# Graph attention on one core: GpSimd multiplies the mask into the last chunk of every other unit, and the projection beside the second attention takes its steps in another order

## The chip, the cores and the metric

The kernel runs on one core of a Trainium2 chip. A core has five engines that run at the same time, each with its own queue in program order: TensorE (PE; its weight loads are listed as PEld), VectorE (DVE), ScalarE (ACT), GpSimd (POOL) and SyncE (SP), which issues transfers. The metric is the device time of one execution in microseconds.

## The reference, cut to what matters

Four layers work on a graph of 3327 nodes with 512 features and a sparse 0/1 matrix `adj`. Layers 0, 2 and 3 are graph attentions with 8 heads of 64 features, layer 1 is a mean over neighbours with dense products. Each starts with a layer norm and ends with a residual sum.

```python
def _L3_gnn_ref(h, adj, W, a):
    hp = jnp.einsum('nd,hdf->hnf', h, W)
    f_src = jnp.einsum('hnf,hf->hn', hp, a_src)
    f_dst = jnp.einsum('hnf,hf->hn', hp, a_dst)
    e = jax.nn.leaky_relu(f_src[:, :, None] + f_dst[:, None, :], ALPHA)
    e = jnp.where(adj[None] > 0, e, NEG_FILL)
    att = jax.nn.softmax(e, axis=-1)
    out = jnp.einsum('hij,hjf->hif', att, hp)
    ...
    return jax.nn.elu(out)

x = x + _L0_gnn_ref(relu(layernorm(x)), adj, ...)   # attention, batch norm
x = x + _L1_gnn_ref(relu(layernorm(x)), adj, ...)   # mean over neighbours
x = x + _L2_gnn_ref(relu(layernorm(x)), adj, ...)   # attention, elu
x = x + _L3_gnn_ref(relu(layernorm(x)), adj, ...)   # attention, elu
```

(The layer norm and relu are written short here.)

## The kernel before, in words

The nodes are padded to 3328, 26 blocks of 128. The kernel first builds, from `adj`, a list of neighbours for each group of 64 target nodes: 52 groups, and for each so many chunks of 128 neighbour indices as the table `CAPS` gives it, 359 chunks in all. Everything after that works on these lists and not on the dense matrix.

A table in device memory holds one row per node: for each head its 64 projected features and a factor (the exponential of its score, so that the sum of weights falls out as a 65th column), and 8 numbers, one per head, for the maximum below. Layer 0's rows also carry the packed edge bits. A second, small array `r_dram` holds the factors of the target nodes.

`attend` runs one attention. It is called three times, for layers 0, 2 and 3; the text calls these the first, second and third attention. It goes through units of two or three chunks (`UNIT` is 3), 135 units in an attention. For each unit:

- `load` (L1165 is the gather in it) issues on GpSimd one indirect transfer per chunk, 128 table rows into the tile `rows`, which has six buffers.
- DVE computes `mx` (L1266): the larger of the target's factor `r_bc`, which TensorE has spread over the partitions in PSUM, and the row's number. 512 elements per partition and chunk: 8 heads by 64 targets. `mx` is a tile in PSUM with one buffer.
- DVE computes `wgt` (L1273): `mx` times the mask, 64 bytes per partition and chunk, the same for all heads. The result is in SBUF and has three buffers.
- TensorE multiplies (L1287): per chunk and head `wgt` transposed by the features, summed in PSUM in `facc` over the group's chunks.
- `later` takes one step of every group that is ending (L1215 copies the sums, L1219 takes reciprocals, L1225 scales the features) and calls `tick`, which takes one or two steps of the work beside the attention.

In the first attention `load` also makes the mask: DVE takes the edge bits out of the gathered rows ("on", L1252) and ACT turns them into 0 and 1 (L1258). The later attentions use the mask that was kept.

The order of PE, DVE and ACT inside `attend` is the program's own (`manual_schedule`); GpSimd isn't in that list, and the only instructions that `attend` gives it are gathers, in the order of the units. A gather waits until TensorE and DVE have finished with the buffer that it overwrites.

Beside the second attention runs the projection of the next layer, `Following.rest`, a generator that `tick` advances, block by block: transposes of the normed rows and `hT` on ACT (L845, L848), the scores `p_sd` (L853) with three ACT operations on them (L857, L858, L860), the clamp of `s_col` on DVE (L863) and the product `p_wh` on TensorE (L866), then `halves` and eight row multiplies on ACT (L870) and the table's row out through SP, then a transpose of `halves`' result (L874), and last its copy `r_row` (L877) and its transfer. `halves` makes two ACT operations (L730, L731) and returns a function that makes a subtraction on DVE (L734). All PSUM tiles of the projection share one buffer (`p_ps`).

Of the kernel before, what the change touches and what calls it, by code (L numbers as in the profile page):

```python
# [23 lines left out]
F32 = mybir.dt.float32  # L24
# [3 lines left out]
I32 = mybir.dt.int32  # L28
# [4 lines left out]
ALU = mybir.AluOpType  # L33
ET = mybir.EngineType
# [4 lines left out]
P = 128  # L39
H = 8  # L40
F = 64
# [9 lines left out]
GB = 64  # L51
# [4 lines left out]
LNB = 5  # L56
ROW = H * (F + 1) + H
UNIT = 3
SUNIT = 2
SROWS = 8  # L60
SAHEAD = 2
SMALL = 53.0
# [662 lines left out]
def halves(nc, pool, cs, sf):  # L725


    rf = pool.tile([P, H], F32, name="r_full", tag="r_full", bufs=2)
    rs = pool.tile([P, 2, H], F32, name="r_half", tag="r_half", bufs=2)
    nc.scalar.activation(rf, sf, AF.Exp, scale=0.8, bias=cs["down"])  # L730
    nc.scalar.copy(rs.bitcast(F32R)[:, 0, :], rf)  # L731

    def other():
        nc.vector.tensor_tensor(rs.bitcast(F32R)[:, 1, :], rf, rs[:, 0, :], ALU.subtract)  # L734
        return rs.rearrange("p t h -> p (t h)")

    return other


class Following:  # L740
# [100 lines left out]
    def rest(self, c, hx):  # L841
        nc, pp, WA, wl = self.tc.nc, self.pool, self.WA, self.wl
        tp = self.psum.tile([P, KC, P], F32, name="p_ps", tag="p_ps", bufs=self.pb)
        for kc in range(KC):
            nc.tensor.transpose(tp[:, kc, :], hx[:, kc * P : (kc + 1) * P], self.cs["ident"])  # L845
        hT = pp.tile([P, KC, P], F32, name="hT", tag="hT", bufs=2)
        for kc in range(KC):
            nc.scalar.activation(hT[:, kc, :], tp[:, kc, :], AF.Relu, accum_out=self.hs[:, c, kc : kc + 1])  # L848
        yield True
        self.mean(c, hT)  # L850
        sd = self.psum.tile([P, BANK], F32, name="p_sd", tag="p_ps", bufs=self.pb)
        for kc in range(KC):
            nc.tensor.matmul(sd[:, : 2 * H], hT[:, kc, :], WA[wl][:, kc, :], start=(kc == 0), stop=(kc == KC - 1))  # L853
        row = pp.tile([P, ROW], F32, name="v_row", tag="v_row", bufs=2)
        V = row[:, : H * (F + 1)].rearrange("p (h f) -> p h f", f=F + 1)
        d = sd[:, H : 2 * H]
        nc.scalar.activation(V[:, :, F : F + 1], d.rearrange("p (h o) -> p h o", o=1), AF.Exp)  # L857
        nc.scalar.activation(row[:, H * (F + 1) :], d, AF.Exp, scale=-0.8, bias=self.cs["down"])  # L858
        sf = pp.tile([P, H], F32, name="s_col", tag="s_col", bufs=2)
        nc.scalar.copy(sf, sd[:, :H])  # L860
        yield True

        nc.vector.tensor_scalar(sf, sf, -SMALL, SMALL, ALU.max, ALU.min)  # L863
        wh = self.psum.tile([P, D], F32, name="p_wh", tag="p_ps", bufs=self.pb)
        for kc in range(KC):
            nc.tensor.matmul(wh, hT[:, kc, :], self.Wt[:, kc, :], start=(kc == 0), stop=(kc == KC - 1))  # L866
        yield True
        rs = halves(nc, pp, self.cs, sf)
        for h in range(H):
            nc.scalar.mul(V[:, h, 0:F], wh[:, h * F : (h + 1) * F], V[:, h, F : F + 1])  # L870
        nc.sync.dma_start(self.table[c * P : (c + 1) * P, :ROW], row.bitcast(I32))
        yield True
        tr = self.psum.tile([2 * H, P], F32, name="p_tr", tag="p_ps", bufs=self.pb)
        nc.tensor.transpose(tr, rs(), self.cs["ident"])  # L874
        yield True
        rr = pp.tile([2 * H, P], F32, name="r_row", tag="r_row", bufs=2)
        nc.scalar.copy(rr, tr)  # L877
        n = P // GB
        nc.sync.dma_start(
            self.r_dram[c * n : (c + 1) * n, :, :, :].rearrange("g t h i -> (t h) g i"),  # L880
            rr.rearrange("h (g i) -> h g i", i=GB),
        )
        yield None
# [253 lines left out]
def sparse(ctx: ExitStack, tc: tile.TileContext, t: dict, out: bass.AP, WA, ls, cs, idx, rdeg, first):  # L1137
# [5 lines left out]
    nc = tc.nc  # L1143
# [18 lines left out]
    mask = keep.tile([P, NCH, GB], U8, name="mask")  # L1162
# [7 lines left out]
    def attend(layer, table, r_dram, finish, tick=lambda: None, home=None):  # L1170
# [5 lines left out]
        units = []  # L1176
        for g in range(ls.G):
            mine = list(ls.batches(g, UNIT))
            units += [(g, k0, n, i == 0, i == len(mine) - 1) for i, (k0, n) in enumerate(mine)]
        hq = H // PG  # L1180
        sw = hq * (F + 1)
        with tc.tile_pool(name=f"fatt{layer}", bufs=2) as ap, tc.tile_pool(
            name=f"facc_ps{layer}", bufs=2, space=PSUM
        ) as aps, tc.manual_schedule(engines={ET.PE, ET.DVE, ET.Activation}):
            rows, rrs, rbs, accs, ends = {}, {}, {}, {}, []

            def fetch(g):
# [43 lines left out]
            def later():  # L1231
                for e in list(ends):
                    if next(e, 0) == 0:
                        ends.remove(e)
                tick()
# [4 lines left out]
            def load(i):  # L1240

                if i >= len(units):
                    return
                g, k0, n, _, _ = units[i]
                gi = ap.tile([P, UNIT, width], I32, name="rows", tag="rows", bufs=6)
                rows[i] = gi.bitcast(F32)
                for k in range(n):
                    gather(gi[:, k, :], table, k0 + k)
                if layer == 0:
                    nw = GB // WB  # L1250
                    on = ap.tile([P, UNIT, nw, WB], U16, name="on", tag="on")
                    nc.vector.tensor_tensor(  # L1252
                        on[:, :n],
                        gi[:, :n, ROW:].bitcast(U16)[:, :, g * nw : (g + 1) * nw].unsqueeze(3).to_broadcast([P, n, nw, WB]),
                        cs["bit"].unsqueeze(1).unsqueeze(1).to_broadcast([P, n, nw, WB]),
                        ALU.bitwise_and,
                    )
                    nc.scalar.activation(mask[:, k0 : k0 + n, :], on[:, :n].rearrange("p k w b -> p k (w b)"), AF.Sign)  # L1258

            load(0)  # L1260
            for i, (g, k0, n, begins, stops) in enumerate(units):
                gt = rows.pop(i)
                mk = mask[:, k0 : k0 + n, :]
                full = [P, n, H, GB]
                mx = aps.tile([P, UNIT, H, GB], F32, name="mx", tag="mx", bufs=1)
                nc.vector.tensor_tensor(  # L1266
                    mx[:, :n],
                    rbs[g].unsqueeze(1).to_broadcast(full),
                    gt[:, :n, H * (F + 1) : ROW].unsqueeze(3).to_broadcast(full),
                    ALU.max,  # L1270
                )
                wt = ap.tile([P, UNIT, H, GB], F32, name="wgt", tag="wgt", bufs=3)
                nc.vector.tensor_tensor(wt[:, :n], mx[:, :n], mk.unsqueeze(2).to_broadcast(full), ALU.mult)  # L1273
                load(i + 1)
                later()
                if begins:
                    fetch(g + 2)
                    acc = aps.tile([P, BANK], F32, name="facc", tag="acc")
                    accs[g] = acc
                    spread(g + 1)  # L1280

                for k in range(n):
                    f, l = begins and k == 0, stops and k == n - 1
                    for q in range(hq):
                        for v in range(PG):
                            h = q * PG + v
                            nc.tensor.matmul(  # L1287
                                accs[g][v * GB : (v + 1) * GB, q * (F + 1) : (q + 1) * (F + 1)],
                                wt[:, k, h, :],
                                gt[:, k, h * (F + 1) : (h + 1) * (F + 1)],  # L1290
                                start=(f and q == 0),
                                stop=(l and q == hq - 1),
                            )
                if stops:
                    ends.append(ending(g))
# [34 lines left out]
    with ExitStack() as mx:  # L1330
# [150 lines left out]
        def tick():  # L1481
            for e in list(ends):
                if next(e, 0) == 0:
                    ends.remove(e)
            proj.tick()
# [3 lines left out]
        for b in range(NB):  # L1489
            ps = list(zip_longest(*(list(ls.batches(b * PG + u, SUNIT)) for u in range(PG))))  # L1490
            parts += [(b, p, i == 0, i == len(ps) - 1) for i, p in enumerate(ps)]
        loaded = {}

        def load(i):
# [3 lines left out]
            for u, kn in enumerate(parts[i][1]):  # L1498
                if kn is not None:
                    k0, n = kn  # L1500
                    zt = gp.tile([P, SUNIT, D], F32, name="z_rows", tag="z_rows", bufs=SROWS)
                    mf = gp.tile([P, SUNIT, GB], F32, name="z_mask", tag="z_mask", bufs=SROWS)
                    nc.scalar.copy(mf[:, :n, :], mask[:, k0 : k0 + n, :])  # L1503
# [7 lines left out]
        for i, (b, _, begins, stops) in enumerate(parts):  # L1511
# [4 lines left out]
            for r, u, k, m, z in loaded.pop(i):  # L1516
# [3 lines left out]
                g = b * PG + u  # L1520
# [102 lines left out]
```

## Time and profile before

| what | value |
| --- | --- |
| runs | 2900.37, 2915.10, 2917.88 us; median 2915.1 us |
| profiled execution, its own time | 2553.76 us |
| its span, first to last instruction | 2551.8 us |
| mean granted TensorE clock in it | 0.851 |
| busy PE, DVE, ACT, POOL | 1825.0, 1852.3, 1068.3, 1387.4 us |

The profiled execution was shorter than the runs beside it; sums made from its rows are compared with its own time. Its rows name a line, an engine, an operation, the tile written and the tiles read, and then a count, the busy time and the mean in ns, and the idle time of that engine just ahead of these instructions with what ended it ("issue": nothing that the profile shows). In the table by stretches the columns are the stretch and its length, then busy time and count for PE, weight loads, DVE, ACT and POOL, the granted clock, the share of the DMA engines and GB/s. In a timeline they are start, duration, engine, line and instruction, and in brackets the idle time before it.

### The profile page before, as it was taken

What the parts mean: (1) busy time and instruction counts of PE and PEld (TensorE: products, weight loads), DVE (VectorE), ACT (ScalarE), POOL (GpSimd) and SP (SyncE); (2) the same over time, 40 slices, a digit from 0 to 9 for tenths busy, and PEclk for the clock granted to TensorE, in tenths of its full rate; (3) what the DMA queues carried; (4) which work ended last, traced back from release to release, by engine and by line L of the source; (5) the groups of instructions that cost most, each with busy time, mean ns of one, the idle gap of its engine ahead of it and who ended that gap; (6) DMA issues with size and microseconds to landing.
All of it is one profiled execution on the core that took longest, in us unless ns stands there. A gap on an engine that the chain in (4) does not pass through costs nothing.

```text
span 2551.8 us, 53690 instructions
## 1 busy us (share of the span) xinstructions
PE 1825.0 (72%) x21112; PEld 1161.8 (46%) x21112; DVE 1852.3 (73%) x2272; ACT 1068.3 (42%) x3810; POOL 1387.4 (54%) x1482
## 2 busy tenths in 40 slices
PE   3667756776677698889999657778878646566653
PEld 2444444454454342223333356656555435555543
DVE  7667579999997850222333499999877279999996
ACT  4553212333445332334455214667766601233444
POOL 1000176777772026777777277776554067777672
PEclk9767889988888899999999778897877787777787
DMA  8773198888783566788888478887665178888784
GB/s 326 288 263 123 43 296 276 280 281 260 241 253 95 191 217 198 234 247 260 254 267 255 125 223 242 235 240 232 199 200 177 39 215 232 236 238 243 232 238 123
DMA packets 189057, 562.57 MB, mean 220 GB/s; under 512 B 37764, under 2 KB 42304, under 8 KB 185470
## 3 DMA queue, kind: packets, MB, share of 16 engines
q0 software_dynamic: 115456, 404.86, 53.3%
q1 hardware_dynamic: 73342, 154.20, 17.0%
q8 instruction: 169, 2.77, 0.4%
q14 instruction: 90, 0.74, 0.1%
HBM read 499.26 MB, written 59.68 MB: 219 GB/s over the span
## 4 chain that ended last, share of the span: by engine, by line
PE 30%; DVE 24%; issue 13%; ACT 9%; DMA 8%; POOL 3%; DVEq 0%; SPq 0%; POOLq 0%; ACTq 0%
DVE mx L1266 12%; PE facc L1287 8%; DVE wgt L1273 8%; PE sage_acc L1522 4%; DMA z_rows<-h_dram,idx 4%; PE p_wh L866 4%; DMA rows<-table,idx 3%; PE n_ps L1471 3%; PE p_wh L808 3%; ACT fhp L1225 2%; POOL z_rows L1165 2%; PE s_ps L1445 2%; POOL rows L1165 1%; ACT bn_y L1225 1%; ACT v_row L870 1%
## 5 line engine op out<-in xcount | busy, mean ns | idle before, releaser
L1165 POOL DMA_INDIRECT rows<-table,idx x1077 | 1027.7, 954 | 580.0 <-issue 224.5
L1287 PE MATMUL facc<-rows,wgt 128*64 128x65 f32 x17232 | 722.5, 253 | 393.7 <-DVE wgt L1273 259.7
L1287 PEld LDWEIGHTS facc<-rows,wgt 128*64 128x64 f32 x17232 | 667.1, 165 | 518.2 <-DVE wgt L1273 310.5
L1266 DVE TENSOR_TENSOR mx<-r_bc,rows 128x1536 f32<-128x1536 f32 (+1 forms) x405 | 639.4, 1579 | 48.4 <-DMA fin_x<-fx 17.7
L1273 DVE TENSOR_TENSOR wgt<-mx,mask 128x1536 f32<-128x1536 f32 (+1 forms) x405 | 638.4, 1576 | 42.3 <-DVE mx L1266 1.0
L1165 POOL DMA_INDIRECT z_rows<-h_dram,idx x359 | 340.7, 949 | 273.7 <-ACT hT L1442 141.0
L1225 ACT ACTIVATE fhp<-sums,rd 64x64 f32<-64x64 f32 x832 | 219.9, 334 | 305.4 <-DVE rd L1219 302.0
L1522 PE MATMUL sage_acc<-z_rows,z_mask 128*64 128x512 f32 x718 | 209.8, 618 | 33.0 <-DMA z_rows<-h_dram,idx 32.6
L1258 ACT ACTIVATE mask<-on 128x192 uint8<-128x192 uint16 (+1 forms) x135 | 46.5, 345 | 325.3 <-DVE on L1252 321.8
L1086 POOL DMA_DIRECT2D list_b<-shift x12 | 6.0, 503 | 271.7 <-DVE shift L1040 271.5
L811 DVE TENSOR_TENSOR sd_pr<-p_wh,ab 128x1024 f32<-128x1024 f32 x26 | 31.8, 1225 | 141.4 <-PE p_wh L808 141.4
L1522 PEld LDWEIGHTS sage_acc<-z_rows,z_mask 128*64 128x64 f32 x718 | 52.2, 137 | 156.2 <-issue 77.6
L680 PE MATMUL wh_ps<-fWt,hT 128*128 128x512 f32 x208 | 123.3, 748 | 0.0
L866 PE MATMUL p_wh<-fWt,hT 128*128 128x512 f32 x208 | 117.2, 714 | 1.4 <-ACT s_col L860 1.4
L1225 ACT ACTIVATE bn_y<-sums,rd 64x64 f32<-64x64 f32 x416 | 109.5, 333 | 2.4 <-DVE rd L1219 0.5
L1503 ACT CAST z_mask<-mask 128x128 f32<-128x128 uint8 (+1 forms) x196 | 52.7, 284 | 118.7 <-PE sage_acc L1522 117.5
L1476 DVE TENSOR_TENSOR s_o<-n_ps,bn_y 128x512 f32<-128x512 f32 x26 | 17.9, 690 | 116.2 <-PE n_ps L1471 116.2
L1215 ACT COPY sums<-facc 128x260 f32<-128x260 f32 x156 | 56.6, 363 | 104.7 <-DMA rows<-table,idx 77.7
L1471 PE MATMUL n_ps<-fWx,aT 128*128 128x512 f32 x208 | 98.7, 608 | 0.0
L808 PE MATMUL p_wh<-fWt,hT 128*128 128x512 f32 x208 | 96.9, 610 | 2.0 <-DVE hT L699 1.9
L1445 PE MATMUL s_ps<-fWx,hT 128*128 128x512 f32 x208 | 93.5, 603 | 3.4 <-ACT hT L1442 3.4
L1198 PE MATMUL r_bc<-r_two,fones 2*128 2x512 f32 x156 | 89.1, 575 | 6.6 <-DMA r_two<-r_dram 3.6
(213 smaller groups left out, 2146.3 us busy)
## 6 DMA issues: line engine op xcount, KB each, us to landing
adj_i<-in_adj SPq DMA_DIRECT2D x26, 1664.0 KB
table<-v_row SPq DMA_DIRECT2D x78, 264.0 KB
rows<-table,idx POOLq DMA_INDIRECT x1077
fin_x<-fx SPq DMA_DIRECT2D x52, 256.0 KB
ln_x<-in_x SPq DMA_DIRECT2D x26, 256.0 KB
bn_x<-in_x SPq DMA_DIRECT2D x13, 512.0 KB
fx<-bn_x SPq DMA_DIRECT2D x13, 512.0 KB
fsage_x<-fx SPq DMA_DIRECT2D x26, 256.0 KB
```

The source lines that it names most:

```text
L680: nc.tensor.matmul(wh, hT[:, kc, :], self.Wt[:, kc, :], start=(kc == 0), stop=(kc == KC - 1))
L808: nc.tensor.matmul(wh, hT[:, kc, :], self.Wt[:, kc, :], start=(kc == 0), stop=(kc == KC - 1))
L866: nc.tensor.matmul(wh, hT[:, kc, :], self.Wt[:, kc, :], start=(kc == 0), stop=(kc == KC - 1))
L1165: nc.gpsimd.indirect_dma_start(out=dst, out_offset=None, in_=src[:, :], in_offset=bass.IndirectOffsetOnAxis(ap=idx[:, k : k + 1], axis=0))
L1198: nc.tensor.matmul(rb, ones[0:2, :].bitcast(F32R), rrs.pop(g).bitcast(F32R), start=True, stop=True)
L1225: nc.scalar.mul(hp[o0 : o0 + GB, h * F : (h + 1) * F], sm[mine, q, 0:F], rd[mine, q, :])
L1266: nc.vector.tensor_tensor(mx[:, :n], rbs[g].unsqueeze(1).to_broadcast(full), gt[:, :n, H * (F + 1) : ROW].unsqueeze(3).to_broadcast(full), ...
L1273: nc.vector.tensor_tensor(wt[:, :n], mx[:, :n], mk.unsqueeze(2).to_broadcast(full), ALU.mult)
L1287: nc.tensor.matmul(accs[g][v * GB : (v + 1) * GB, q * (F + 1) : (q + 1) * (F + 1)], wt[:, k, h, :], gt[:, k, h * (F + 1) : (h + 1) * (F + 1)],
L1445: nc.tensor.matmul(ps, hT[:, kc, :], Wx[:, 0, kc, :], start=(kc == 0), stop=(kc == KC - 1))
L1471: nc.tensor.matmul(ps, aT[:, kc, :], Wx[:, 1, kc, :], start=(kc == 0), stop=(kc == KC - 1))
L1522: nc.tensor.matmul(acc[u * GB : (u + 1) * GB, :], m, z, start=f, stop=l)
```

## The change

It does two things. In `attend`, for every unit with an odd number, the last chunk's maximum is written by DVE into `wgt` directly, and GpSimd multiplies it there by the mask, of which ACT has made an fp32 copy (`mask_f`) one unit ahead. The other chunks of that unit go through `mx` and `wgt` on DVE as before. GpSimd's instructions in `attend` are now in the program's own order. The gathers of three units (`AHEAD`) are issued before the first unit, and those of unit i + 3 at the beginning of unit i. The making of the mask is cut out of `load` and stays where `load(i + 1)` was.

In `Following.rest`, which runs beside the second attention, the work of a block is cut differently: the clamp of `s_col` goes behind the product, `halves` behind the row multiplies, its subtraction gets a step alone, and the transpose goes into the step of `r_row`.

```diff
+AHEAD = 3
...
         yield True
-
-        nc.vector.tensor_scalar(sf, sf, -SMALL, SMALL, ALU.max, ALU.min)
         wh = self.psum.tile([P, D], F32, name="p_wh", tag="p_ps", bufs=self.pb)
         for kc in range(KC):
             nc.tensor.matmul(wh, hT[:, kc, :], self.Wt[:, kc, :], start=(kc == 0), stop=(kc == KC - 1))
         yield True
-        rs = halves(nc, pp, self.cs, sf)
+
+        nc.vector.tensor_scalar(sf, sf, -SMALL, SMALL, ALU.max, ALU.min)
         for h in range(H):
             nc.scalar.mul(V[:, h, 0:F], wh[:, h * F : (h + 1) * F], V[:, h, F : F + 1])
         nc.sync.dma_start(self.table[c * P : (c + 1) * P, :ROW], row.bitcast(I32))
+        rs = halves(nc, pp, self.cs, sf)
+        yield True
+        rs = rs()
         yield True
         tr = self.psum.tile([2 * H, P], F32, name="p_tr", tag="p_ps", bufs=self.pb)
-        nc.tensor.transpose(tr, rs(), self.cs["ident"])
-        yield True
+        nc.tensor.transpose(tr, rs, self.cs["ident"])
         rr = pp.tile([2 * H, P], F32, name="r_row", tag="r_row", bufs=2)
         nc.scalar.copy(rr, tr)
...
-        ) as aps, tc.manual_schedule(engines={ET.PE, ET.DVE, ET.Activation}):
+        ) as aps, tc.manual_schedule(engines={ET.PE, ET.DVE, ET.Activation, ET.Pool}):
...
-                if layer == 0:
+
+            def edges(i):
+
+                if layer == 0 and i < len(units):
+                    g, k0, n, _, _ = units[i]
+                    gi = rows[i].bitcast(I32)
...
-            load(0)
+            mps = {}
+
+            def widened(i):
+
+                if i < len(units) and i % 2:
+                    _, k0, n, _, _ = units[i]
+                    mp = mps[i] = ap.tile([P, GB], F32, name="mask_f", tag="mask_f", bufs=3)
+                    nc.scalar.copy(mp, mask[:, k0 + n - 1, :])
+
+            for i in range(AHEAD):
+                load(i)
+            edges(0)
             for i, (g, k0, n, begins, stops) in enumerate(units):
+                load(i + AHEAD)
                 gt = rows.pop(i)
                 mk = mask[:, k0 : k0 + n, :]
+                wt = ap.tile([P, UNIT, H, GB], F32, name="wgt", tag="wgt", bufs=3)
+
+                if i % 2:
+                    n -= 1
+                    one = [P, H, GB]
+                    nc.vector.tensor_tensor(
+                        wt[:, n], rbs[g], gt[:, n, H * (F + 1) : ROW].unsqueeze(2).to_broadcast(one), ALU.max
+                    )
+                    nc.gpsimd.tensor_tensor(wt[:, n], wt[:, n], mps.pop(i).unsqueeze(1).to_broadcast(one), ALU.mult)
+                    mk = mk[:, :n, :]
                 full = [P, n, H, GB]
                 mx = aps.tile([P, UNIT, H, GB], F32, name="mx", tag="mx", bufs=1)
...
-                wt = ap.tile([P, UNIT, H, GB], F32, name="wgt", tag="wgt", bufs=3)
                 nc.vector.tensor_tensor(wt[:, :n], mx[:, :n], mk.unsqueeze(2).to_broadcast(full), ALU.mult)
-                load(i + 1)
+                edges(i + 1)
                 later()
+                widened(i + 1)
...
+                n = units[i][2]
                 for k in range(n):
```

## The prediction

> **What bounds the kernel now.** I read four things in this order: the page's slices, the groups by line, the engines' timelines inside one attention stage, and the waits of the second attention. The slices first.
>
> ```profile
> DVE  7667579999997850222333499999877279999996
> POOL 1000176777772026777777277776554067777672
> ```
>
> Slices are 63.8 us. In slices 5 to 12, 22 to 30 and 32 to 39, the three attentions, VectorE (DVE) is at nine tenths and GpSimd (POOL) seems to have a quarter of its time free. The table by stretches says the same, in the page's order PE, weight loads, DVE, ACT, POOL:
>
> ```profile
> 319.00:800.00 481.00, 325.29 (x5892) 237.20 (x5892) 451.48 (x457) 168.65 (x593) 341.28 (x359) 0.87 0.83 263
> 1447.00:1985.00 538.00, 404.89 (x6117) 309.90 (x6117) 470.30 (x476) 304.57 (x1180) 342.63 (x359) 0.80 0.73 216
> 2046.00:2552.00 506.00, 285.05 (x5796) 251.31 (x5796) 461.24 (x374) 158.15 (x520) 343.75 (x359) 0.77 0.76 221
> ```
>
> So 359 gathers in each attention and a DVE with 30 to 68 us idle. The groups give the price of the pieces: the two DVE operations of a unit at 1536 (three chunks) and 1024 elements (two), and the gather.
>
> ```profile
> L1165 POOL DMA_INDIRECT rows<-table,idx x1077 | 1027.7, 954 | 580.0 <-issue 224.5 <-PE facc L1287 149.9 <-DMA r_two<-r_dram 111.6
> L1266 DVE TENSOR_TENSOR mx<-r_bc,rows 128x1536 f32<-128x1536 f32 x267 | 470.1, 1761 | 47.3 <-DMA fin_x<-fx 17.7 <-DMA rows<-table,idx 13.3 <-PE r_bc L1198 11.5
> L1266 DVE TENSOR_TENSOR mx<-r_bc,rows 128x1024 f32<-128x1024 f32 x138 | 169.3, 1227 | 1.2
> ```
>
> The reader is to stop at "issue 224.5" in the first row: idle time in which GpSimd waited for nothing. The timeline of GpSimd in the third attention shows what it is:
>
> ```profile
> 2213.67 1.23 DVE L1273 TENSOR_TENSOR wgt<-mx,mask 128x1024 f32<-128x1024 f32 x1
> 2214.81 0.17 DVE L1219 RECIPROCAL rd<-sums 128x4 f32<-128x4 f32 x1
> 2214.99 1.77 DVE L1266 TENSOR_TENSOR mx<-r_bc,rows 128x1536 f32<-128x1536 f32 x1
> ```
>
> ```profile
> 2212.93 0.94 POOL L1165 DMA_INDIRECT rows<-table,idx  x1 [0.30 <-PE facc L1287]
> 2214.18 0.95 POOL L1165 DMA_INDIRECT rows<-table,idx  x1 [0.30 <-DMA rows<-table,idx]
> 2215.43 0.95 POOL L1165 DMA_INDIRECT rows<-table,idx  x1 [0.31 <-PE facc L1287]
> 2216.68 0.95 POOL L1165 DMA_INDIRECT rows<-table,idx  x1 [0.30 <-issue]
> ```
>
> Gathers start every 1.25 us, with a hole of 0.30 or 0.31 us whatever releaser is named. GpSimd runs back to back. The first and last gather of each attention start at 319.43 and 788.18, 1447.72 and 1978.16, 2046.52 and 2513.65: 468.8, 530.4 and 467.1 us, where 358 spacings of 1.25 us make 447.5. The true slack of GpSimd is therefore 21.3, 82.9 and 19.6 us, 123.8 in all. **GpSimd and DVE are both bounds** of the first and third attention, within 5% of each other. In the second, small waits add up:
>
> ```profile
> POOL rows L1165 <- PE facc L1287: 97.8, 67, 5.0
> PE p_ps L845 <- ACT r_row L877: 31.0, 14, 2.5
> DVE s_col L863 <- ACT s_col L860: 20.3, 10, 2.5
> ```
>
> Columns: total us, times, longest. GpSimd stands for buffers there; PE and DVE wait in order for ScalarE (ACT) steps of the next projection.
>
> **What the Trainium skill says.** "Perfetto Trace Analysis", section "GPSIMD Engine Instruction", tells to time such instructions by start-to-start spacing, not by the span shown; the trace agrees (0.95 us shown, 1.25 us spacing). "GPSIMD Engine Reference", section 3.1, gives 4497 ns for a two-input fp32 tensor_tensor of 2048 elements; no run here shows one. "SBUF — State Buffer", section "Who interferes with whom", says that a DVE instruction with two SBUF inputs contends with a GpSimd one that reads SBUF, and one with a single SBUF input doesn't. mx and wgt each read one operand from PSUM; the trace before has no GpSimd arithmetic to show it.
>
> **The change part by part.**
>
> *DVE.* An odd unit of three chunks had 2 x 1.76 = 3.52 us; it becomes one max of 512 elements, and a max and a multiply of 1024. Per 512 elements the rows differ by 0.534 us, so 512 elements cost about 0.69 us (the 128x512 operation at L1318 has 0.693). That makes 0.69 + 2 x 1.23 = 3.15, 0.37 less; two chunks give 2.45 to 2.08, the same. Each attention has 135 units, 67 odd: 201 x 0.37 = 74 us of DVE work less. It helps only where GpSimd isn't later.
>
> *GpSimd.* 201 multiplies of 128x512 stand among the gathers: in the order of GpSimd's queue one multiply follows each five or six gathers. Let c be what one adds to the spacing. Below: the memset of 1664 elements took 1.484 us, so 512 can't well be under 0.46, and c might be that or, with the hole filled, less. Skill's price in proportion (an estimate from that page): 512/2048 x 4.497 = 1.12 us. Above: this and a hole of 0.30, and some blocking, 1.6. I take 1.2. A stage then needs 447.5 + 67 x 1.2 = 527.9 us between first and last gather. Against before: +59.1, -2.5, +60.8, **+117 us**. In general 201c - 124, so it breaks even at c = 0.62.
>
> *Order and waits.* GpSimd is now ordered by hand. Multiply i waits for the first max of unit i on DVE and for ACT's copy of the mask; the gathers of units i+4 and i+5 stand behind it, three units of lookahead where six buffers allowed five before. Those three units are 8 x 1.25 + 1.2 = 11 us. At the start of the second attention rows took 3.2 us from the end of the third gather's issue to their use (1451.2 to 1454.35), in the first, under load, 7.3 (322.98 to 330.25). A DVE faster than GpSimd has done that max by then: I cost the wait at nothing in the first and third attention, and the cover is DVE's new idle time of about 90 us a stage. TensorE waits for GpSimd only before a unit's last chunk, behind 2.45 us of DVE work that it waits for anyway. In the second attention ACT may be behind, because its queue contains hT, the row multiplies and r_row that wait for PE: 0 to 2.5 us (the longest such wait above) for each of 26 blocks; I take 0.5: +13 us.
>
> *ACT.* 201 copies of 64 elements, 0.24 us each by the z_mask cast of that size (L1503, 241 ns): 16 us a stage on an engine with at least 230 us free. Nothing; without that cover 48 us. The edge bits ("on" and the mask's Sign) keep their place behind the multiply of the unit before: nothing.
>
> *DVE against GpSimd.* The two-input ones are "on" in the first attention (135, 0.33 us) and L1318 and L1319 (52 each, 0.69). They fill below a tenth of a stage; 67 multiplies x 0.1 x 0.5 us is 3 us a stage. In the bounds of c.
>
> *The projection's steps.* The clamp of s_col moves one step later, ACT's r_full and r_half go behind the eight row multiplies, the subtraction gets a step alone, and PE's transpose joins ACT's r_row copy and its DMA on SP. No instruction is added, and SP keeps its order (table, then r_dram). This takes away about 20 us of DVE and up to 31 us of PE waiting in the second attention; GpSimd at 527.9 + 13 us covers that gain, so I count nothing for it. r_row leaves no later, so the drain before the third attention stays.
>
> Sum: 117 + 13 = **+130 us**, on the profiled execution's own 2553.8 us (span 2551.8): 2684. The median of the runs shown is 2915.1, which is 361 us or 14% above it, and no view tells where. Unscaled, 3045; in proportion, 2915.1 x (1 + 130/2553.8) = 3063. I say **3050**.
>
> **Rivals.**
> 1. *The holes take the multiply, faster.* Five gathers have 1.6 us of holes, enough for a multiply of 1.12 us. If GpSimd's arithmetic can fill them, c is near 0 and DVE's relief counts down to the gathers' 447.5 us: -21, -20 and, of the second's 83, about 50 (25 of DVE work, 20 of s_col, some of p_ps): -91, or 2825. For it: GpSimd's busy share of 0.68 to 0.71. Against: the 0.30 is there with nothing to wait for, so it belongs to issuing. It decides below c = 0.62.
> 2. *In-order stalls.* The multiply often waits for ACT or DVE in the second attention and holds the gathers: 26 x 2.5 = 65 us in place of 13, +182, scaled 3120. For it: 51 us of ACT waiting for p_wh there. Against: three units of lookahead.
> 3. *The unprofiled runs are bound elsewhere.* If their 361 us lie partly in TensorE (granted clock 0.74 to 0.87 here in the attentions), a longer stage hides most of 80 us of multiplies: 2915 to 2960. For it: only the gap between the two times.
> 4. *The change doesn't do what it says*: excluded, the multiplies stand in GpSimd's queue.
>
> **How the numbers follow.** Forecast 0.67 (c from 0.9 to 1.6 gives +70 to +211: 2985 to 3156 with scaling), rival 1 0.09, rival 2 0.12, rival 3 0.12, half of it within 1%. About 1% is what a measurement of this kernel tells from no change. Faster 0.09, same 0.07 (half of rival 3 and a little of the forecast's low end), slower 0.84. Range 2930 to 3160: it leaves out rival 1 and the ends of 2 and 3.
>
> **What would show it.** Right: gathers still 1.25 us apart, a multiply adding 0.9 to 1.6 us after five or six of them; first to last gather about 528, 541 and 528 us; DVE idle on rows or on PE some 80 us in each attention; s_col's wait gone. Wrong: GpSimd idle before the multiplies for many microseconds (rival 2), multiplies that leave the gathers' spacing as it was (rival 1), or attentions of unchanged length.

## The result and the profile after

Four runs of the changed kernel have a median of 2944.83 us (2941.32 to 2957.78), four of the kernel before 2916.49 us (2900.37 to 2918.11). The ratio is 1.0129, with a 95% interval of 1.0101 to 1.0157: slower, by a fifth to a third of what was forecast. The profiled execution of the changed kernel took 2957.78 us, so this time the profile is of an execution like those that are timed.

The chain of waits of the kernel before, from its first page, and then the page of the changed kernel, its chain and the groups that answer to those shown before:

```profile
PE 30%; DVE 24%; issue 13%; ACT 9%; DMA 8%; POOL 3%; DVEq 0%; SPq 0%; POOLq 0%; ACTq 0%
```

```profile
PE 44%; issue 12%; ACT 6%; DVE 4%; another core or an unknown queue 1%; DMA 1%; POOL 1%; SPq 0%; DVEq 0%; ACTq 0%; POOLq 0%
...
L1167 POOL DMA_INDIRECT rows<-table,idx x1077 | 1042.5, 968 | 531.1 <-issue 230.2
L1317 PE MATMUL facc<-rows,wgt 128*64 128x65 f32 x17232 | 999.2, 270 | 455.7 <-issue 425.0
...
L1291 POOL TENSOR_TENSOR wgt<-wgt,mask_f 128x512 f32<-128x512 f32 x201 | 256.7, 1277 | 116.9 <-ACT mask_f L1274 106.9
L1288 DVE TENSOR_TENSOR wgt<-r_bc,rows 128x512 f32<-128x512 f32 x201 | 138.3, 688 | 245.4 <-PE facc L1317 160.2
...
L1259 DVE TENSOR_TENSOR on<-rows,fbit 128x192 uint16<-128x192 uint16 (+1 forms) x135 | 105.6, 782 | 13.2 <-DMA rows<-table,idx 13.2
```

Three things are new against the first profile. The chain that sets the end is TensorE's: 44% against 30% in the first profile, with DVE down from 24% to 4%. TensorE's products for facc have 425 us of idle time put down to "issue". And DVE waits for TensorE (160 us ahead of the first max alone), not for rows. Run e1 below shows that none of the three is the change's doing: the kernel before has them too when its profile is of a longer execution.

GpSimd in the third attention of the changed kernel, the timeline:

```profile
2601.59 0.94 POOL L1167 DMA_INDIRECT rows<-table,idx  x1 [0.30 <-DVE mx L1295]
2602.55 1.28 POOL L1291 TENSOR_TENSOR wgt<-wgt,mask_f 128x512 f32<-128x512 f32 x1
2603.99 1.26 POOL L1167 DMA_INDIRECT rows<-table,idx  x1 [0.16 <-PE facc L1317]
2605.56 0.95 POOL L1167 DMA_INDIRECT rows<-table,idx  x1 [0.30 <-issue]
```

From gather to gather with a multiply between them it is 2.40 us, where it is 1.25 without: the multiply adds 1.15 us to the spacing. The prediction's c, what one multiply adds, was 1.2.

### The profile page after: what moved, and what is told of

Its sections match the earlier page's. It is cut to its first block, busy times and chain, and to the rows that moved or that the text cites. A ratio compares the mean times of both kernels' runs of the same rounds, so it can differ in the third digit from the quotient of the medians.

```text
span 2956.0 us, 54775 instructions
## 1 busy us (share of the span) xinstructions
PE 2144.6 (73%) x21112; PEld 1360.4 (46%) x21112; DVE 1847.8 (63%) x2473; ACT 1110.0 (38%) x4011; POOL 1660.4 (56%) x1683
## 4 chain that ended last, share of the span: by engine, by line
PE 44%; issue 12%; ACT 6%; DVE 4%; another core or an unknown queue 1%; DMA 1%; POOL 1%; SPq 0%; DVEq 0%; ACTq 0%; POOLq 0%
PE facc L1317 20%; PE sage_acc L1552 5%; PE p_wh L865 4%; PE p_wh L809 3%; PE n_ps L1501 3%; PE s_ps L1475 3%; PE r_bc L1200 2%; PE p_sd L854 1%; ACT fhp L1227 1%; ACT v_row L870 1%; PE p_ps L801 1%; ACT hT L849 1%; PE p_ps L846 1%; PE var_ps L1435 1%
## 5 line engine op out<-in xcount | busy, mean ns | idle before, releaser
L1167 POOL DMA_INDIRECT rows<-table,idx x1077 | 1042.5, 968 | 531.1 <-issue 230.2
L1317 PE MATMUL facc<-rows,wgt 128*64 128x65 f32 x17232 | 999.2, 270 | 455.7 <-issue 425.0
L1317 PEld LDWEIGHTS facc<-rows,wgt 128*64 128x64 f32 x17232 | 843.1, 178 | 679.5 <-issue 612.2
L1301 DVE TENSOR_TENSOR wgt<-mx,mask 128x1024 f32<-128x1024 f32 (+2 forms) x405 | 531.2, 1312 | 96.5 <-PE facc L1317 49.4
L1295 DVE TENSOR_TENSOR mx<-r_bc,rows 128x1024 f32<-128x1024 f32 (+2 forms) x405 | 530.5, 1310 | 30.9 <-DMA rows<-table,idx 27.4
L1291 POOL TENSOR_TENSOR wgt<-wgt,mask_f 128x512 f32<-128x512 f32 x201 | 256.7, 1277 | 116.9 <-ACT mask_f L1274 106.9
L1288 DVE TENSOR_TENSOR wgt<-r_bc,rows 128x512 f32<-128x512 f32 x201 | 138.3, 688 | 245.4 <-PE facc L1317 160.2
L865 PE MATMUL p_wh<-fWt,hT 128*128 128x512 f32 x208 | 119.8, 728 | 1.9 <-ACT s_col L861 1.4
L809 PE MATMUL p_wh<-fWt,hT 128*128 128x512 f32 x208 | 107.8, 666 | 16.9 <-ACT hT L804 10.9
L1259 DVE TENSOR_TENSOR on<-rows,fbit 128x192 uint16<-128x192 uint16 (+1 forms) x135 | 105.6, 782 | 13.2 <-DMA rows<-table,idx 13.2
```

The lines of the kernel that those rows point to most:

```text
L1167: nc.gpsimd.indirect_dma_start(out=dst, out_offset=None, in_=src[:, :], in_offset=bass.IndirectOffsetOnAxis(ap=idx[:, k : k + 1], axis=0))
L1259: nc.vector.tensor_tensor(on[:, :n], gi[:, :n, ROW:].bitcast(U16)[:, :, g * nw : (g + 1) * nw].unsqueeze(3).to_broadcast([P, n, nw, WB]), ...
L1288: nc.vector.tensor_tensor(wt[:, n], rbs[g], gt[:, n, H * (F + 1) : ROW].unsqueeze(2).to_broadcast(one), ALU.max)
L1291: nc.gpsimd.tensor_tensor(wt[:, n], wt[:, n], mps.pop(i).unsqueeze(1).to_broadcast(one), ALU.mult)
L1295: nc.vector.tensor_tensor(mx[:, :n], rbs[g].unsqueeze(1).to_broadcast(full), gt[:, :n, H * (F + 1) : ROW].unsqueeze(3).to_broadcast(full), ...
L1317: nc.tensor.matmul(accs[g][v * GB : (v + 1) * GB, q * (F + 1) : (q + 1) * (F + 1)], wt[:, k, h, :], gt[:, k, h * (F + 1) : (h + 1) * (F + 1)],
```

## The experiments

After the result I held two theories. **A**: in the executions that are timed TensorE bounds the attentions, the stages are longer than in the first profile, and GpSimd's multiplies mostly fit into them. **B**: GpSimd bounds them as predicted, and something gave the time back. All ratios are to the kernel before on the same chip. It took 2916 us beside the result, and 2959, 2954 and 2957 us beside e1 to e4, e5 to e8 and e9 to e12, three groups that each ran on a chip of their own; so the ratios count, and microseconds are best compared within a group. The measure of a stage is the time from its first to its last gather, read from one profile of each run. Two profiles of the changed kernel (the result's and e9's) differ by 6, 10 and 11 us in the three attentions: differences of that size in a stage show nothing by themselves.

**e1, the kernel before once more**, without an edit.

> The kernel before, unchanged, profiled once more. Theory A (TensorE's instructions arrive too slowly in the runs that are timed, and this bounds the attentions and the mean over neighbours): about 2915 us with a profile of nearly the same span, in which TensorE's row for facc shows 400 us or more of idle time put down to issue where the first profile had 98, and the mean over neighbours takes some 560 us in place of 477. Theory B (GpSimd bounds the attentions, as predicted): a profile near 2552 us again, gathers 1.25 us apart without a pause; the gap of 361 us to the timed runs stays unexplained.

Measured: 2957.65 us, ratio 1.0008 (0.9986 to 1.0029), profiled at 2957.11 us. None of its 20 runs was under 2939, none of 54 more of the same kernel under 2935: 2554 us didn't come back. Here are the row of TensorE's products in the first profile, and then two groups of this page:

```profile
L1287 PE MATMUL facc<-rows,wgt 128*64 128x65 f32 x17232 | 722.5, 253 | 393.7 <-DVE wgt L1273 259.7
```

```profile
L1165 POOL DMA_INDIRECT rows<-table,idx x1077 | 1027.1, 954 | 881.5 <-PE facc L1287 384.7
L1287 PE MATMUL facc<-rows,wgt 128*64 128x65 f32 x17232 | 988.9, 270 | 423.3 <-issue 395.3
```

GpSimd isn't back to back here: it waits 385 us for TensorE to give back buffers, against 150 in the first profile. TensorE for its part waited mostly for DVE in the first profile, and here almost only for "issue". Its timeline in the third attention, first of the first profile and then of this one, shows what holds it:

```profile
2300.97 2.87 PE L1287 MATMUL facc<-rows,wgt 128*64 128x65 f32 x48 [0.75 <-DVE wgt L1273]
...
2304.66 2.87 PE L1287 MATMUL facc<-rows,wgt 128*64 128x65 f32 x48
```

```profile
2511.55 1.38 PE L1287 MATMUL facc<-rows,wgt 128*64 128x65 f32 x37 [1.10 <-issue]
2513.33 0.39 PE L1287 MATMUL facc<-rows,wgt 128*64 128x65 f32 x5 [0.40 <-issue]
2514.08 0.38 PE L1287 MATMUL facc<-rows,wgt 128*64 128x65 f32 x5 [0.37 <-issue]
2514.84 0.40 PE L1287 MATMUL facc<-rows,wgt 128*64 128x65 f32 x6 [0.38 <-issue]
2516.28 1.79 PE L1287 MATMUL facc<-rows,wgt 128*64 128x65 f32 x27 [1.05 <-issue]
```

In the first profile the 48 matmul instructions of a unit of three chunks run in a row (an fp32 product takes two of them: e5 below makes the same products in bf16 with half as many). In e1 there are now 37 in a row, now five or six and a hole, the next batch 0.75 us later, and nothing is shown that TensorE waits for. The stages by this profile, beside the first one and the changed kernel's:

| first to last gather, us | first attention | mean over neighbours | second | third |
| --- | --- | --- | --- | --- |
| before, first profile | 468.8 | 472.5 | 530.4 | 467.1 |
| before, e1 | 571.1 | 578.1 | 628.6 | 566.7 |
| after | 572.4 | 558.1 | 651.1 | 561.9 |

Theory A fits this profile: its chain of waits is TensorE's for 56%, and all four stages, the mean over neighbours too, are 98 to 106 us longer. e5 and e8 test it. The prediction's slack of 123.8 us was read from the first row; the second one has 571.1 + 628.6 + 566.7 - 3 x 447.5 = 424 us. And against e1, which ran on another chip, the changed kernel's second attention is 22 us longer and the other two nearly the same.

**e2, the steps alone**: `rest` of the changed kernel in the kernel before.

> Only the projection's steps are changed. Theory A: TensorE bounds the second attention, so waits of DVE on s_col are mostly covered: 2895 to 2915 us. Theory B: GpSimd has 83 us of slack in that stage, and half of the waits go: 2865 to 2895 us.

Measured: 2966.08 us, 1.0029 (1.0011 to 1.0047); second attention 629.7. The steps bring nothing, not even the little that either theory allowed; if anything they cost 0.3%.

**e3, attend alone**: the changed kernel with the old `rest`.

> Only attend is changed: GpSimd's multiplies, its order and three units of lookahead, with the projection's steps as before. Theory A: 2945 us like the whole change, or up to 30 us more if the old steps and the multiply's wait for ACT's mask copy add up. Theory B: at least 3000 us; the steps gave back what the multiplies cost.

Measured: 2994.21 us, 1.0131 (1.0080 to 1.0183); stages 575.2, 653.7 and 574.7. In ratio this is the whole change's loss; B's 3000 us is nearly met only because this chip's base is 2959. The loss is in attend. Against e1, on the same chip, the second attention is 25 us longer, the first and third 4 and 8.

**e4, the order without the multiplies**:

```diff
-                if i % 2:
+                if i % 2 > 1:
                     n -= 1
```

(and the same in `widened`).

> The whole change without the multiplies: no unit hands a chunk to GpSimd, but GpSimd is in the program's order with three units of lookahead, and the projection has its new steps. Theory A with the loss in the multiplies' waits: 2900 to 2915 us, as before. Theory A with the loss in the shorter lookahead: 2940 us. Theory B: 2890 to 2915 us.

Measured: 2968.63 us, 1.0036 (1.0017 to 1.0054); stages 573.4, 638.1 and 568.9. This is less than the 2940 us (1.009) that a loss in the lookahead would have given. The run has the new steps too, which alone measured 1.0029 in e2, so the order by itself isn't shown to cost anything; most of the loss comes with the multiplies. "on" has a mean of 328 ns here, 330 in e1 and 782 in the changed kernel.

**e5 and e6, TensorE relieved**: products for facc in bf16, in the kernel before and in the changed one. This lowers the precision of the attention's products.

```diff
-                wt = ap.tile([P, UNIT, H, GB], F32, name="wgt", tag="wgt", bufs=3)
+                wt = ap.tile([P, UNIT, H, GB], BF16, name="wgt", tag="wgt", bufs=3)
...
-                                gt[:, k, h * (F + 1) : (h + 1) * (F + 1)],
+                                gt[:, k, :].bitcast(BF16)[:, 1::2][:, h * (F + 1) : (h + 1) * (F + 1)],
```

In e6 DVE's first max goes to an fp32 tile of its own, from which GpSimd multiplies into `wgt`.

> The kernel before with the products for facc in bf16: wgt is written as bf16, and TensorE reads the upper half of each fp32 feature. The same products are made, at lower precision, with half as many instructions on TensorE (8616 in place of 17232 matmuls); DVE, ACT, GpSimd and all transfers stay. Theory A (TensorE's instructions bound the attentions in the timed runs): the three attentions fall from 569, 637 and 567 us between first and last facc product to 470, 545 and 475, as in the first profile, and the whole to 2670 us. Rival (the timed runs are slower everywhere, or in the transfers): above 2850 us.

> The changed kernel with the same bf16 products. Theory A with the prediction's sum behind it: with TensorE out of the way GpSimd bounds the attentions, 447.5 + 67 x 1.2 to 1.4 = 528 to 541 us between first and last gather, so this is 110 to 160 us slower than the kernel before with bf16 products, 2780 to 2830 us. Rival (GpSimd's multiplies hide in any case): within 30 us of it.

Measured: e5 2832.20 us, 0.9588 (0.9550 to 0.9626); e6 2864.90 us, 0.9722 (0.9679 to 0.9764). Stages of e5 536.5, 577.0 and 535.6, of e6 539.0, 599.0 and 537.7. So half of TensorE's instructions for facc take 31 to 52 us off each attention: they do bound it. The granted clock was lower in both runs (a mean of 0.68, against 0.78 in e1), so a higher clock isn't what shortened the stages. But the fall to 470 us didn't come, and 2832 us lies far nearer to the rival's 2850 than to the 2670 of theory A; e5's groups still have TensorE in front:

```profile
L1287 PE MATMUL facc<-rows,wgt 128*64 128x65 bf16 x8616 | 425.3, 236 | 689.0 <-issue 532.4
```

The holes don't go with the number of instructions, and both of my sums for this pair were wrong: e5 gained less than the sum said, and e6 is 33 us slower than e5, not 110 to 160, close to the rival's 30. At 536 us a stage GpSimd's work of 447.5 + 67 x 1.15 = 525 us still just fits. That the limit is near shows in the waits of e6, a row that the changed kernel has with 2.0 us:

```profile
PE facc L1318 <- POOL wgt L1292: 130.6, 46, 5.7
```

**e7, the mask copies earlier**:

```diff
                 edges(i + 1)
+                widened(i + 1 if layer == 0 else i + 3)
                 later()
-                widened(i + 1)
```

(with `widened(1)` ahead of the loop in the later attentions).

> The whole change, but ACT makes the fp32 mask copies of the second and third attention two units earlier, and all of them before the steps of the work beside. Theory C (what is lost is lost where a multiply waits for the copy in the second attention, and the gathers behind it): waits of GpSimd on mask_f fall from 107 us to under 20, the second attention gets 15 to 25 us shorter, 1.003 to 1.007 of the kernel before. Rival D (the loss is in the order, the lookahead or in DVE against GpSimd): 1.010 to 1.015, like the whole change.

Measured: 2979.58 us, 1.0084 (1.0051 to 1.0117); stages 578.0, 639.1 and 574.7. GpSimd's waits in the second attention, of the changed kernel and of e7:

```profile
POOL wgt L1291 <- ACT mask_f L1274: 101.0, 30, 9.5
...
POOL rows L1167 <- PE facc L1317: 38.5, 52, 2.8
```

```profile
POOL rows L1167 <- PE facc L1319: 81.1, 72, 3.8
...
POOL wgt L1293 <- ACT fhp L1227: 28.0, 14, 3.7
POOL wgt L1293 <- DVE wgt L1290: 14.5, 5, 7.9
```

The 101 us, 30 waits of up to 9.5 us in which the next gathers stand behind a multiply that lacks its mask, are gone. Most of it comes back as other waits: 43 us more for TensorE's buffers, 28 for another operation of ACT and 15 for DVE. The stage is 12 us shorter than the changed kernel's and 22 us shorter than e9's, both measured on other chips. The ratio lies between theory C's 1.003 to 1.007 and rival D's 1.010 to 1.015: theory C names the right wait, but its removal gave back only a part of the loss. e12 below repeats this beside e9, on the same chip.

Why the copy is late, ACT's own waits in that stage of the changed kernel show:

```profile
ACT v_row L870 <- PE p_wh L865: 74.6, 19, 9.2
ACT v_row L858 <- PE p_sd L854: 35.4, 17, 6.0
```

ACT works through its queue in order, and there the copies of the mask stand behind operations of the projection that wait for TensorE.

**e8, every multiply twice**:

```diff
-                    nc.gpsimd.tensor_tensor(wt[:, n], wt[:, n], mps.pop(i)...
+                    mp = mps.pop(i)
+                    for _ in range(2):
+                        nc.gpsimd.tensor_tensor(wt[:, n], wt[:, n], mp...
```

> The whole change with every multiply by the mask made twice on GpSimd (the mask is 0 or 1, so the result is the same). GpSimd then needs 447.5 + 134 x 1.3 = 622 us a stage. If the multiplies only just fit beside TensorE, as 569 us of stage against 535 to 541 us of work say: 50 to 60 us more in the first and third attention, 30 to 60 in the second, 1.05 to 1.07 of the kernel before. If GpSimd has slack that its spacing doesn't show: 1.015.

Measured: 3114.56 us, 1.0552 (1.0514 to 1.0591); stages 617.4, 689.2 and 622.7, against 622 expected for a stage that GpSimd bounds. Its timeline is back to back again:

```profile
2601.39 0.94 POOL L1167 DMA_INDIRECT rows<-table,idx  x1 [0.30 <-issue]
2602.34 2.64 POOL L1293 TENSOR_TENSOR wgt<-wgt,mask_f 128x512 f32<-128x512 f32 x2
2605.12 0.98 POOL L1167 DMA_INDIRECT rows<-table,idx  x1
```

3.73 us from gather to gather, 2.48 for two multiplies. So the sum for GpSimd was sound, and the first 67 multiplies of a stage were nearly free because they filled the time that TensorE left.

**e9 to e12, on one chip**: the changed kernel again; multiplies in the first and third attention only (`layer != 2` added to both conditions); in the second only (`layer == 2`); and e7 with `AHEAD = 4`.

> The changed kernel once more, beside the next three on the same chip: 1.013 of the kernel before, as measured; first to last gather about 572, 652 and 568 us.

> The whole change, but in the second attention no unit hands a chunk to GpSimd. If the multiplies cost nothing in the first and third attention, where 538 us of GpSimd's work fit into 569 us, and all of the loss in the second: 1.002 to 1.006, as with the order alone. If they cost their share in each: 1.009.

> The whole change, but only the second attention's odd units hand a chunk to GpSimd. Loss in the second attention alone: 1.010 to 1.015, all of the change's loss. Loss spread evenly: 1.006.

> The early mask copies, and the gathers of four units ahead in place of three. If the second part of the loss comes from the shorter lookahead (the order alone made the second attention 9 us longer): 1.002 to 1.006. If the lookahead doesn't matter: 1.008, as with the early copies alone.

| | median, us | ratio (95% interval) | first | second | third attention, us |
| --- | --- | --- | --- | --- | --- |
| e9 | 3007.39 | 1.0175 (1.0120 to 1.0229) | 578.4 | 661.4 | 573.2 |
| e10 | 2973.64 | 1.0055 (1.0033 to 1.0078) | 577.5 | 629.4 | 573.3 |
| e11 | 3000.04 | 1.0156 (1.0107 to 1.0205) | 574.5 | 659.7 | 567.8 |
| e12 | 2982.03 | 1.0089 (1.0059 to 1.0118) | 576.2 | 639.9 | 572.7 |

The second attention loses some 30 us by its multiplies (661.4 or 659.7 against 629.4), and the medians agree: without them the kernel is 34 us faster (e10 against e9). The first and third are 3 and 5 us longer with multiplies (e10 against e11), and the whole is 7 us longer (e9 against e11); these differences are within what two profiles, or the intervals, leave open. e9 is the changed kernel again, and its loss reads 1.75% here, 1.3% in the result. A fourth unit of lookahead shows no gain over e7 (1.0089 against 1.0084).

e12 against e9 is the early copy on one chip, with one more unit of lookahead. The multiplies' waits for the mask in the whole run, of e9 and of e12:

```profile
POOL wgt L1291 <- ACT mask_f L1274: 112.3, 38, 8.7
```

```profile
POOL wgt L1293 <- ACT mask_f L1274: 3.7, 1, 3.7
```

With them gone the kernel is 25 us faster, and the intervals just don't overlap. So about half of the 50 us that e9 loses is the wait for the copy. The other half is in pieces too small for these intervals to tell apart: 0.3% that the steps alone read, and what the multiplies cost otherwise in the three attentions.

The fastest version of all is e5, at 0.9588, but it trades precision for it. Of those that keep fp32 none beat the kernel before.

## Why the prediction was wrong

The direction was right and the range held the time, but the loss was 28 us (1.3%), not 135 (4.6%).

- **The step that failed is the first one**: "GpSimd and DVE are both bounds" of the first and third attention, and the 123.8 us of "true slack" that came of it. They were read correctly from an execution of 2554 us, while the runs shown were 361 us longer. e1 and e5 show that in such runs TensorE bounds the attentions; the three are 98 to 102 us longer there, and GpSimd has 424 us of slack. In the sum 201c - 124 the 124 was the wrong term. With 424 it gives 241 - 424, below nothing: GpSimd's own work isn't what the change costs. e8, with twice the work, brings the predicted bound back. The prediction had this as its third rival, with the right range (2915 to 2960), at 0.12, and it named TensorE; it thought of the granted clock, where the trace shows holes. It asked where the 361 us were and went on without an answer; the likeliest case of a timed run should have been built on the timed runs.
- *The price of a multiply* was right: c = 1.2 taken, 1.15 measured (1.24 in e8). The multiplies did not disappear in the holes of 0.30 us (rival 1); a multiply follows a gather without its hole and leaves one of 0.16.
- *The order of the queue*, the term of 13 us, had the right mechanism in the right place and was too small: copies of the mask stand in ACT's queue behind work that waits for TensorE, and the multiply and the gathers behind it wait. The term was 0.5 us for 26 blocks, at most 2.5. That 2.5 us was read from the wrong rows: they are waits of TensorE and DVE for ACT. ACT's own waits stood in the same view of the kernel before, more and longer:

```profile
ACT v_row L870 <- PE p_wh L866: 51.2, 21, 5.4
ACT hT L848 <- PE p_ps L845: 36.4, 23, 5.9
ACT v_row L857 <- PE p_sd L853: 32.2, 16, 4.1
```

  Measured were 30 waits of up to 9.5 us and 101 us of GpSimd idle in that stage. Its second rival, at 0.12, put such waits at 65 us and took all of them to reach the end; but GpSimd isn't the bound, and 25 us of the whole kernel's time come back when the copy is early (e12 against e9). This wait is the largest single piece of the loss that was found.
- *The stages*: the sum had +59, +11 and +61 us for the three attentions. On one chip the second is 25 (e3 against e1) to 32 us (e9 against e10) longer by the change in attend, the first and third 0 to 8. That the time fell within the range is no support for the sum: the range was wide enough to hold nearly all of the third rival, and the third rival is what came.
- *DVE's relief* of 74 us: the three groups of max and multiply went from 1278.0 us (e1: 639.6 + 638.4) to 1200.0 (530.5 + 531.2 + 138.3). But "on" took 61 us more, so DVE's total fell from 1856.1 to 1847.8 us only. The prediction gave such collisions 3 us a stage. It doesn't show in the time, since DVE waits for TensorE.
- *The steps* counted at nothing: e2 shows no gain either, and perhaps a loss of 0.3%. The wait of DVE on s_col did fall, from 56.8 us in e1 to 5.9.

## What to carry to other kernels

When the profiled execution is shorter than the runs by more than their spread, its slack and its bound need not be those of the runs: first say what the missing time is, and if that can't be said, give the case "bound elsewhere" the most weight. Work moved to an engine with a queue in order costs little while it fits into the stage, and then its price is the wait that it puts ahead of the work behind it: ask what its last input waits for, and make that input early. Doubling the moved work helps to tell slack from a bound in one run.

## What was not expected of the hardware

- One execution of the kernel before took 2554 us, 113 others 2900 to 2980. In the longer ones TensorE's instructions come in batches of a few, with holes in which it waits for nothing shown. In e1's three attentions TensorE and its weight loads stand still together 842 times for over 0.1 us ahead of a facc instruction without a wait, 381 us in all, and 484 times a new batch starts 0.70 to 0.80 us after the one before. In the first profile there are 45 such holes, 95 us in all, and no two within 3 us. Granted clocks differ too (0.851 against 0.78 as a mean), but 473 of e1's holes stand in stretches granted the full clock and 369 in stretches granted half: the table by stretches has 1.00 for 2500.0 to 2502.4 us of e1, in which TensorE ran 10 matmul instructions. What makes the holes was not found; the packets that load instructions on the largest such queue took as long in both (median 964 and 982 ns in the two traces), and with half the instructions (e5) the holes stayed.
- DVE's "on", with both inputs in SBUF, rose from a mean of 330 ns (e1) to 782, up to 2.14 us, where GpSimd multiplies of 1.28 us run; without the multiplies (e4) it was 328. Its larger form in e1, to be held against the changed kernel's row above:

```profile
L1252 DVE TENSOR_TENSOR on<-rows,fbit 128x192 uint16<-128x192 uint16 x89 | 31.2, 351 | 11.7 <-DMA rows<-table,idx 11.7
```

  All 48 that took over 0.45 us overlap a multiply in the trace, and 3 of the other 87 do. The Trainium skill's "SBUF — State Buffer", section "Who interferes with whom", says that a DVE instruction with two SBUF inputs contends with a GpSimd one that reads SBUF; these numbers agree. The longest took more than a multiply's 1.28 us and their own 0.35 together, and the trace doesn't say why. mx and wgt, with one input in PSUM, kept their 1.76 and 1.23 us, as the same section has it.
- The two-input multiply of 512 fp32 elements took 1.28 us on GpSimd, 14% above the 1.12 us that I had estimated from "GPSIMD Engine Reference", section 3.1, in proportion. What it added to the spacing of the gathers was 1.15 us.
